# A four-layer selective-scan stack: how the other batch element's steps are dealt out between the scans

## Chip, cores and metric

The kernel runs on one core of a Trainium2 chip. The metric is the device time of one launch in microseconds (us); the time before is the median of three runs. All arithmetic is float32.

## What is computed

Four layers follow each other on x of shape (4, 64, 64, 128): batch, height, width, channels. Layers 0, 1 and 3 are selective-scan blocks, layer 2 is a gated block. Cut to what matters, with L = 4096 positions, DI = 256, N = 16 and four scan directions k (rows, columns, and both backwards):

```
selective-scan block (layers 0, 1, 3)
  xx, z = split(norm(x) @ in_proj)                # 128 -> 256 + 256
  xx    = silu(conv3x3_depthwise(xx) + b)
  for k in 4:  dt, B, C = x_proj[k] @ xs[k];  dt = softplus(dt_w[k] @ dt + b)
               h[t] = exp(dt[t]*A) * h[t-1] + dt[t]*xs[t]*B[t]        # 256 x 16 states
               y[k][t] = sum over n of h[t]*C[t]
  y = sum of y[k], turned back into place, + D * xs
  x = x + (norm(y) * silu(z)) @ out_proj
  x = x + gelu(norm(x) @ fc1 + b) @ fc2 + b       # 128 -> 512 -> 128
gated block (layer 2)
  s = (norm(x) @ w1 + b1) * wdw + bdw;  s = s1 * s2
  s = s * (mean over positions(s) @ wse + bse);   x = x + beta * (s @ w2 + b2)
  c = norm(x) @ wf1 + bf1;                        x = x + gamma * ((c1 * c2) @ wf2 + bf2)
```

## The kernel before, in words

**Turns, chunks, periods.** Elements of the batch go in pairs. While the scans of one element run, everything that is not a scan (norms, projections, convolution, MLP, gated block) is done for the other. There are 12 turns (L709 to L712: element, layer). A turn has 4 directions of 8 chunks of 512 positions, so 32 chunks, and a chunk has 8 periods; the whole is 3072 periods. A period does 4 of the 32 scans of a chunk (16 states for two halves of 128 channels).

**The steady work of a period** is written out by hand in the loop of `scans` (L935 on). In program order: two `da` on ScalarE for the next period (L854, the exponential), two scans on VectorE from `dbp` (L870), the product with C on GpSimd (`hc`, L882) and on every other period a sum of two of them (L884), TensorE's sum over states into `yp` (L895, two or four matmuls, of the period before), TensorE's `dbp` of the next period (L845, four matmuls of 256 columns), two more `da`, then twice a product `dbv` (L984) and a scan on VectorE, a copy `dup` (L862) every other period, and four `diag` on ScalarE (L837) from which a later `dbp` is made. SyncE's queue carries all DMAs; `bb` and `cb`, the rows of B and C, are loaded every other period (L821). PSUM is full: `dbp` has one buffer of two banks, so the next `dbp` can only be written when both its scans are done, and the other element's work has one bank, `gap`.

**Prologue.** The next chunk is prepared by the generator `prologue` (L761 to L814) in ten pieces at fixed half periods (`PIECES`). The piece in the fifth period holds both softplus activations and two table loads on ScalarE.

**The other element's steps.** `between` (L197 on) makes a list of small closures: each issues the instructions of one engine, as a rule. A norm is `mean` (matmul, L226), `centre` (VectorE, L230), `square` (ScalarE, L234), `variance` (matmul, L238), `root` (ScalarE, L241 and L242), `scale` (VectorE, L245), `affine` (ScalarE, L252). The output norm over 256 channels is the same at L338 to L361, `project_z` is L378 to L385, the convolution is nine matmuls for each half (`taps`, L402) with a ScalarE `take` (L413), then `silu` (L421), `gate` on GpSimd (L445), `project` (L450), `add` (L453), the MLP (`up` L477, `take` L480, `gelu` L485, `down` L495, `add` L500), and for the gated layer `product` on GpSimd (L589) and `total` on VectorE (L592). `rest()` puts empty steps (L210) between a producer and its consumer. `later(fn, n)` puts a store n steps further on. In the four turns in which the other element goes through layer 2 (`gated`), three taps make one step:

```python
            stride = 3 if gated else 1
```

**Pacing.** Each period has four places at which `other(number)` issues steps: 0 after the first scan, 1 after the prologue's piece in the middle, 2 after the third scan, 3 at the end. A segment is a list of steps with a first and a last place. Every step counts one, empty ones too, and every place of the segment has the same share:

```python
                gone = at % (8 * per_turn) * 4 + number
                for todo, count, frm, to in segments:
                    while todo and count - len(todo) < count * (gone - frm) / (to - frm):
                        todo.pop(0)()
```

A turn's segment runs from its third period to four places before its 31st chunk (`meanwhile`, L736); so in the last two chunks of a turn nothing of the other element is issued. The first six chunks of the first turn and the last ones of the last turn have a segment for each chunk. What is left at the end is issued after the loop.

Of the kernel before, what the change touches and what calls it, by code (L numbers as in the profile page):

```python
# [58 lines left out]

VSS_AT, VSS_N = _columns(_VSS)  # L60
GATE_AT, GATE_N = _columns(_GATE)


@with_exitstack
def vss_stack_kernel(ctx: ExitStack, tc: tile.TileContext, x: bass.AP, weights, out: bass.AP, n_batch=B, layers=(0, 1, 2, 3)):
# [90 lines left out]
    def combine(i, psums):  # L156

        S = []
        z = SimpleNamespace()

        def load():
            z.in_w = gap1.tile([P, DI], F32, tag="cen", name="in_w")
            nc.sync.dma_start(out=z.in_w, in_=weights[i][0][:, :DI])

        def turn(m):
            z.ps = psums[0].tile([P, CH], F32, tag="gap", name="gap")
            nc.tensor.transpose(z.ps[:, :P], z.in_w[:, m * P : (m + 1) * P], ident)

        def take():
            z.in_t = gap1.tile([P, P], F32, tag="sq", name="in_t")  # L170
            nc.scalar.copy(z.in_t, z.ps[:, :P])

        def taps(m, t, count):
            z.taps = gap1.tile([P, 4, P], F32, tag="t", name="taps")
            for j in range(count):
                nc.scalar.activation(z.taps[:, j], ident, AF.Copy, scale=wt[i]["conv_w"][:, m, t + j : t + j + 1])

        def project(count):
            z.ps = psums[0].tile([P, CH], F32, tag="gap", name="gap")
            for j in range(count):  # L180
                nc.tensor.matmul(z.ps[:, j * P : (j + 1) * P], z.in_t, z.taps[:, j], start=True, stop=True)

        def leave(m, t, count):
            conv = gap1.tile([P, 4 * P], F32, tag="y", name="conv")
            nc.scalar.copy(conv[:, : count * P], z.ps[:, : count * P])
            at = (m * 9 + t) * P
            nc.sync.dma_start(out=conv_d[i][:, at : at + count * P], in_=conv[:, : count * P])

        S.append(load)
        for m in range(2):  # L190
            S.extend((partial(turn, m), take))
            for t in range(0, 9, 4):
                count = min(4, 9 - t)
                S.extend((partial(taps, m, t, count), partial(project, count), partial(leave, m, t, count)))
        return S

    def between(e, frm, to, psums):  # L197
# [9 lines left out]

        def rest(n=pause):

            S.extend([lambda: None] * n)  # L210

        def later(fn, n=3):

# [7 lines left out]

        def norm(src, dst, wgt, bias, eps):

            def mean():
                z.ps = bank()
                nc.tensor.matmul(z.ps, mean128, src(), start=True, stop=True)  # L226

            def centre():
                z.cen = gap1.tile([P, CH], F32, tag="cen", name="cen")
                nc.vector.tensor_sub(z.cen, src(), z.ps)  # L230

            def square():
                z.sq = gap1.tile([P, CH], F32, tag="sq", name="sq")
                nc.scalar.activation(z.sq, z.cen, AF.Square)  # L234

            def variance():
                z.ps = bank()
                nc.tensor.matmul(z.ps, mean128, z.sq, start=True, stop=True)  # L238

            def root():  # L240
                nc.scalar.activation(z.ps, z.ps, AF.Ln, bias=eps)  # L241
                nc.scalar.activation(z.ps, z.ps, AF.Exp, scale=-0.5)  # L242

            def scale():
                nc.vector.tensor_mul(z.cen, z.cen, z.ps)  # L245

            def affine():
                to_sb = dst()
                cen = z.cen
                if len(to_sb.shape) == 3:  # L250
                    cen = cen.rearrange("p (h w) -> p h w", w=W)
                nc.scalar.activation(to_sb, cen, AF.Identity, scale=wgt, bias=bias)  # L252

            S.append(mean)
            rest()
            S.extend((centre, square))
            rest(1)
# [51 lines left out]
        def begin(c):  # L309


            def turn():
# [12 lines left out]
            later(lambda: nc.sync.dma_start(out=lane.res[:, cols(c)], in_=z.res))  # L325

        def output_norm(c):
            if to is None:
                S.append(lambda: fetch(c))
                rest(2)  # L330

            def mean():
# [10 lines left out]
            def square():  # L343
                z.wide = gap1.tile([P, 4, CH], F32, tag="wide", name="wide")
                nc.scalar.activation(z.wide[:, 0:2], z.y, AF.Square)

            def variance():
# [25 lines left out]
            S.append(affine)  # L373

        def project_z():
            def first():
                z.ps = bank()
                nc.tensor.matmul(z.ps, z.in_z[:, :P], z.xn, start=True, stop=True)  # L378

            def second():  # L380
                z.ps = bank()
                nc.tensor.matmul(z.ps, z.in_z[:, P:], z.xn, start=True, stop=True)
# [5 lines left out]

        def convolve(c):

            stride = 3 if gated else 1
            for m in range(2):
                for first in range(0, 9, stride):

                    def taps(m=m, first=first):
                        if m == 0 and first == 0 and (frm is None or gated):
                            z.wide = gap1.tile([P, 4, CH], F32, tag="wide", name="wide")
# [45 lines left out]
        def mixer_out(c):  # L443
            def gate():
                nc.gpsimd.tensor_mul(z.y, z.y, z.wide[:, 0:2])  # L445

            def project():
                z.ps = bank()
                for m in range(2):
# [15 lines left out]
        def mlp(c, store):  # L465
# [4 lines left out]
            norm(lambda: z.res, fresh, v["n2w"], v["n2b"], eps5)  # L470
            for j in range(4):

                def up(j=j):
                    if j == 0:
                        z.wide = gap1.tile([P, 4, CH], F32, tag="wide", name="hid")
# [13 lines left out]
            rest(1 + breath)  # L489
            for j in range(4):  # L490

                def down(j=j):
                    if j == 0:
                        z.ps = bank()
# [48 lines left out]
            later(store, 2)  # L543

        def finish(c):
            def turn():
                z.ps = bank()
                for j in range(4):
# [13 lines left out]
        def gate_sums(c):  # L562
# [6 lines left out]

            norm(lambda: z.res, fresh, g["n1w"], g["n1b"], eps6)  # L570

            def first():
                z.ps = bank()
                nc.tensor.matmul(z.ps, g["w1"][:, :P], z.t, start=True, stop=True)

            def take():
                z.g1 = gap1.tile([P, CH], F32, tag="cen", name="g1")
                nc.scalar.activation(z.g1, z.ps, AF.Identity, scale=g["wdw"][:, 0:1], bias=g["cb"][:, 0:1])

            def second():  # L580
                z.ps = bank()
                nc.tensor.matmul(z.ps, g["w1"][:, P:], z.t, start=True, stop=True)
# [16 lines left out]
        def attention():  # L599
            g = wt[2]  # L600

            def mean():
                z.mean = gap1.tile([P, 1], F32, tag="mean", name="mean")
                nc.vector.tensor_reduce(z.mean, z.sums, AX.X, ALU.add)
                nc.vector.tensor_scalar_mul(z.mean, z.mean, 1.0 / L)

            def se():
                z.ps = bank()
                nc.tensor.matmul(z.ps[:, 0:1], g["wse"], z.mean, start=True, stop=True)
# [10 lines left out]
        def gate_rest(c):  # L620
            g = wt[2]

            def project():
                z.s, z.res = z.next_s, z.next_res
                z.ps = bank()
# [14 lines left out]
            rest(2)  # L640
            norm(lambda: z.res, fresh, g["n2w"], g["n2b"], eps6)

            def first():
                z.ps = bank()
                nc.tensor.matmul(z.ps, g["wf1"][:, :P], z.t, start=True, stop=True)

            def take():
                z.c1 = gap1.tile([P, CH], F32, tag="cen", name="c1")
                nc.scalar.activation(z.c1, z.ps, AF.Identity, bias=g["bf1"][:, 0:1])

            def second():
                z.ps = bank()
                nc.tensor.matmul(z.ps, g["wf1"][:, P:], z.t, start=True, stop=True)

            def both():
                z.c2 = gap1.tile([P, CH], F32, tag="sq", name="c2")
                nc.vector.scalar_tensor_tensor(z.c2, z.ps, g["bf1"][:, 1:2], z.c1, ALU.add, ALU.mult)

            def down():
                z.ps = bank()  # L660
                nc.tensor.matmul(z.ps, g["wf2"], z.c2, start=True, stop=True)
# [94 lines left out]
    def scans(pool, ring, deep, psum):  # L756
# [178 lines left out]
        for at, (s, i) in enumerate(periods):  # L935
            then = periods[at + 1] if at + 1 < len(periods) else None
            if i == 0:
# [2 lines left out]
                    pro, nxt.dt = prologue(nxt), s.dt  # L940
                s.state = pool.tile([P, 2, N], F32, tag="state", name="state") if s.first else before[0].state
                if at % (8 * per_turn) == 0:
                    segments = [(steps, len(steps), frm, to) for steps, frm, to in meanwhile(s.turn)]

            def piece(number):

# [2 lines left out]

            def other(number):  # L950

                gone = at % (8 * per_turn) * 4 + number
                for todo, count, frm, to in segments:
                    while todo and count - len(todo) < count * (gone - frm) / (to - frm):
                        todo.pop(0)()

            da_next = [None, None]
            spreads = (s, i // 2 + 1) if i < 7 else (nxt, 0)
# [46 lines left out]
            da = da_next  # L1005
            before = (s, i)
            if then and then[0].turn != s.turn:
                assert not any(todo for todo, *_ in segments)
# [5 lines left out]
        for todo, *_ in segments:  # L1014
            for step in todo:
                step()

    with (
# [91 lines left out]
```

## Time and profile before

| | us |
|---|---|
| median of three runs (23297.77 to 23323.02) | 23302.88 |
| the profiled execution, its own time | 23325.13 |
| its span, first to last instruction | 23323.4 |
| GpSimd busy | 19260.3 (83%) |
| ScalarE busy | 18075.1 (77%) |
| scans with `dbp` / with `dbv`, mean of one | 1.259 / 1.280 |
| `hc` product on GpSimd, mean of one | 2.361 |
| mean of a period (span without start and end / 3072) | 7.5 |
| mean granted TensorE clock | 0.956 |

The span stretches from the first to the last instruction; the profiled execution's own time is 1.7 us more, and 22 us (0.1%) over the median. A float32 matmul shows as two records. In the views of waits a line says which engine waited with which instruction, what released it, and then the time in total, how often, and the longest.

### The profile page before, as it was taken

To read this page: it belongs to the slowest core of one execution; us is meant where nothing else is said; L and a number is where in the kernel's file an instruction comes from. 1 tells how busy PE (TensorE), PEld (TensorE's weight loads), DVE (VectorE), ACT (ScalarE), POOL (GpSimd) and SP (SyncE) were. 2 spreads that over 40 slices of the span, in tenths; PEclk is the share of its full clock that TensorE was granted. 3 is DMA by queue.
4 is the path that set the end of the run, shared out by engine and by line. 5 is a ranking of instruction groups with operands and counts; after the bars stand their busy time and mean duration, and the time that the engine had idled before them with its cause. 6 is when DMAs were issued, how large, how long until landed. Compare 5 with 4: busy or idle time off the path is not lost. (4 is left out here: it accounts for less than half of the span.)

```text
span 23323.4 us, 216855 instructions
## 1 busy us (share of the span) xinstructions
PE 20052.7 (86%) x58234; PEld 10604.8 (45%) x58234; DVE 20362.5 (87%) x20186; ACT 18075.1 (77%) x38870; POOL 19260.3 (83%) x8862
## 2 busy tenths in 40 slices
PE   7888888888888888888888888888888888888887
PEld 3444444444444444444444444444444444444443
DVE  5999899988887888898899899898988878888996
ACT  5788787777777787787788787787877777877886
POOL 5898888888887787888888788888888878878885
PEclk8999999999999999999999999999999999999998
DMA  4444444444334434434533544444443443344332
GB/s 104 147 142 144 131 130 145 131 131 140 125 125 126 130 126 126 135 130 134 139 133 130 139 138 132 134 144 127 132 141 122 126 128 131 123 128 136 131 132 101
DMA packets 2437558, 3060.09 MB, mean 131 GB/s; under 512 B 1753840, under 2 KB 1790064, under 8 KB 2238192
## 3 DMA queue, kind: packets, MB, share of 16 engines
q1 hardware_dynamic: 2436336, 3046.22, 42.1%
q8 instruction: 472, 7.73, 0.1%
q14 instruction: 750, 6.14, 0.1%
HBM read 2784.41 MB, written 261.49 MB: 131 GB/s over the span
## 5 line engine op out<-in xcount | busy, mean ns | idle before, releaser
L882 POOL TENSOR_TENSOR hc<-h,cb 128x1024 f32<-128x1024 f32 x6144 | 14420.4, 2361 | 3675.8 <-DVE h L870 2362.9
L895 PE MATMUL yp<-hc,ident 128*128 128x512 f32 x18432 | 9087.0, 620 | 641.9 <-POOL hc L884 395.2
L854 ACT ACTIVATE da<-delta,w 128x512 f32<-128x512 f32 x12288 | 8158.8, 713 | 1557.2 <-DVE h L870 1532.3
L845 PE MATMUL dbp<-diag,duT 128*128 128x256 f32 x24576 | 6276.1, 400 | 1832.3 <-DVE h L870 1729.2
L870 DVE TENSOR_TENSOR_SCAN h<-da,state,dbp 128x512 f32<-128x512 f32 x5376 | 6564.8, 1259 | 939.5 <-PE dbp L845 757.6
L870 DVE TENSOR_TENSOR_SCAN h<-da,state,dbv 128x512 f32<-128x512 f32 x5376 | 6879.6, 1280 | 477.6 <-ACT da L854 11.1
L845 PEld LDWEIGHTS dbp<-diag,duT 128*128 128x128 f32 x24576 | 4740.1, 198 | 4329.2 <-issue 2850.9
L895 PEld LDWEIGHTS yp<-hc,ident 128*128 128x128 f32 x18432 | 3491.1, 198 | 4992.6 <-issue 3633.6
L984 DVE TENSOR_TENSOR dbv<-dup,bb 128x512 f32<-128x512 f32 x6144 | 4226.0, 688 | 614.2 <-ACT dup L862 400.7
L837 ACT ACTIVATE diag<-ident,bt 128x128 f32<-128x128 f32 x12288 | 3947.5, 401 | 0.2
L884 POOL TENSOR_TENSOR hc<-hc 128x1024 f32<-128x1024 f32 x1536 | 3622.5, 2358 | 120.4
L862 ACT COPY dup<-du 128x512 f32<-128x512 f32 x1920 | 1125.3, 586 | 1267.6 <-DVE dbv L984 1231.8
L402 PE MATMUL gap<-halo,cw 128*128 128x512 f32 x3456 | 1658.6, 605 | 15.6 <-ACT wide L413 6.2
L870 DVE TENSOR_TENSOR_SCAN h<-da,dbp 128x512 f32<-128x512 f32 x768 | 892.5, 1200 | 130.8 <-PE dbp L845 104.1
L870 DVE TENSOR_TENSOR_SCAN h<-da,dbv 128x512 f32<-128x512 f32 x768 | 937.3, 1220 | 79.3 <-ACT da L854 14.1
L805 POOL TENSOR_TENSOR du<-delta,xs 128x512 f32<-128x512 f32 x768 | 978.3, 1274 | 33.7 <-ACT delta L793 33.7
L788 PE MATMUL ps_dt<-xd,dt_w 8*128 8x512 f32 x1536 | 887.2, 658 | 124.9 <-ACT delta L791 73.6
L402 PEld LDWEIGHTS gap<-halo,cw 128*128 128x128 f32 x3456 | 642.1, 192 | 743.8 <-issue 700.7
L878 ACT COPY state<-h 128x2 f32<-128x2 f32 x5376 | 960.9, 179 | 0.0
L413 ACT ACTIVATE wide<-gap,w 128x512 f32<-128x512 f32 x192 | 132.1, 688 | 824.2 <-PE gap L402 824.1
L813 ACT COPY duT<-ps_duT 128x512 f32<-128x512 f32 x768 | 440.0, 573 | 181.3 <-PE ps_duT L811 180.5
L791 ACT ACTIVATE delta<-ps_dt,w 128x512 f32<-128x512 f32 x768 | 524.6, 683 | 37.2 <-PE ps_dt L788 32.6
(121 smaller groups left out, 11443.0 us busy)
## 6 DMA issues: line engine op xcount, KB each, us to landing
cb<-xd_d SPq DMA_DIRECT2D x1536, 1024.0 KB
bb<-xd_d SPq DMA_DIRECT2D x1536, 512.0 KB
xs<-x_row_d SPq DMA_DIRECT2D x192, 512.0 KB
xs<-x_col_d SPq DMA_DIRECT2D x192, 512.0 KB
x_col_d<-down SPq DMA_DIRECT2D x192, 256.0 KB
x_row_d<-wide SPq DMA_DIRECT2D x96, 512.0 KB
y_d<-y_sb SPq DMA_DIRECT2D x96, 512.0 KB
y<-y_d SPq DMA_DIRECT2D x96, 512.0 KB
```

Of the source, the lines that this page charges most:

```text
L402: nc.tensor.matmul(z.ps, z.cw[:, m, t, :], z.halo[c][:, dy : dy + RPC, dx : dx + W], start=(t == 0), stop=(t == 8),)
L805: nc.gpsimd.tensor_mul(s.du[:, m], s.delta[:, m], s.xs[:, m])
L837: nc.scalar.activation(s.diag[q][:, t, :, j], ident, AF.Copy, scale=s.bt[:, t, CQ * q + j : CQ * q + j + 1])
L845: nc.tensor.matmul(s.db[:, t * P : (t + 1) * P, :], s.duT[:, t, m, :], s.diag[q][:, t], start=True, stop=True)
L854: nc.scalar.activation(da[:, j], s.delta[:, m], AF.Exp, scale=s.v["a"][:, s.k, m, n : n + 1])
L862: nc.scalar.copy(s.dup, s.du[:, m])
L870: nc.vector.tensor_tensor_scan(s.h[i, side][:, j, s.step], da[:, j, s.step], db[:, s.step], init, ALU.mult, ALU.add)
L878: nc.scalar.copy(s.state[:, m, n : n + 2].unsqueeze(2), s.h[i, side][:, :, s.end : s.end + 1])
L882: nc.gpsimd.tensor_mul(hc, s.h[i, side], s.cb[i // 2][:, 2 * side : 2 * side + 2, :])
L884: nc.gpsimd.tensor_add(hc, hc, s.hc[i, 0])
L895: nc.tensor.matmul(getattr(s, f"yp{m}"), ident, s.hc[i, side][:, j], start=opens and j == 0, stop=i == end and side == 1 and j == 1,)
L984: nc.vector.tensor_mul(db, s.dup, s.bb[i // 2][:, j])
```

## The change

1. A decorator `tensor(n)` marks a step with its number of 512-column matmuls: 1 for `mean`, `variance`, `first`, `second`, `up`, `down` and single taps; 2 for the output norm's `mean` and `variance` and for `project`; 0.6 for four transposes, 0.3 for smaller ones, 0.1 for `se`.
2. A step costs that many; an empty step costs 0.1, any other step 0.25. A segment advances by cost and no longer by number of steps.
3. The places of a chunk no longer have equal shares: the eight periods have the shares of `ROOM`, each spread evenly over its four places.
4. Taps are single steps in all turns (`stride = 1`).
5. At one place a segment issues either steps with matmuls or steps without; when the kind changes it stops until the next place, unless the segment's end has been reached. Empty steps have no kind.

The lists of steps and their order within a segment stay as they were, but for the split taps. The instructions on every engine are the same ones in another order between the scans.

```diff
+ROOM = (0.8, 1.9, 1.0, 0.9, 0.2, 0.4, 0.9, 1.2)
+
+def tensor(matmuls):
+    def mark(fn):
+        fn.matmuls = matmuls
+        return fn
+    return mark
+
+def cost(step):
+    return getattr(step, "matmuls", 0) or (0.1 if step is empty else 0.25)
+
+def when(place):
+    chunk, place = divmod(place, 4 * len(ROOM))
+    i, number = divmod(place, 4)
+    return chunk + (sum(ROOM[:i]) + ROOM[i] * number / 4) / sum(ROOM)
...
-            S.extend([lambda: None] * n)
+            S.extend([empty] * n)
...
+            @tensor(1)
             def mean():
...
-            stride = 3 if gated else 1
+            stride = 1
             for m in range(2):
                 for first in range(0, 9, stride):
+                    @tensor(stride)
                     def taps(m=m, first=first):
...
-                    segments = [(steps, len(steps), frm, to) for steps, frm, to in meanwhile(s.turn)]
+                    segments = [
+                        SimpleNamespace(todo=steps, done=0.0, total=sum(map(cost, steps)), frm=when(frm), to=when(to))
+                        for steps, frm, to in meanwhile(s.turn)
+                    ]
...
-                gone = at % (8 * per_turn) * 4 + number
-                for todo, count, frm, to in segments:
-                    while todo and count - len(todo) < count * (gone - frm) / (to - frm):
-                        todo.pop(0)()
+                gone = when(at % (8 * per_turn) * 4 + number)
+                for g in segments:
+                    last = None
+                    while g.todo and g.done < g.total * (gone - g.frm) / (g.to - g.frm):
+                        step = g.todo[0]
+                        kind = None if step is empty else hasattr(step, "matmuls")
+                        if None not in (kind, last) and kind != last and gone < g.to:
+                            break
+                        last = last if kind is None else kind
+                        g.done += cost(g.todo.pop(0))
+                        step()
```

More of the change, by code (lines that the diff above doesn't have):

```diff
@@ L61, with empty @@
 GATE_AT, GATE_N = _columns(_GATE)
+ROOM = (0.8, 1.9, 1.0, 0.9, 0.2, 0.4, 0.9, 1.2)
[6 more added lines that the diff above has]
+    return getattr(step, "matmuls", 0) or (0.1 if step is empty else 0.25)
+def empty():
+    pass
+def when(place):
+    chunk, place = divmod(place, 4 * len(ROOM))
+    i, number = divmod(place, 4)
+    return chunk + (sum(ROOM[:i]) + ROOM[i] * number / 4) / sum(ROOM)
 @with_exitstack
@@ L190, in combine @@
         for m in range(2):
-            S.extend((partial(turn, m), take))
+            S.extend((tensor(0.3)(partial(turn, m)), take))
             for t in range(0, 9, 4):
                 count = min(4, 9 - t)
-                S.extend((partial(taps, m, t, count), partial(project, count), partial(leave, m, t, count)))
+                S.extend((partial(taps, m, t, count), tensor(0.3 * count)(partial(project, count)), partial(leave, m, t, count)))
         return S
@@ L234, in square @@
                 nc.scalar.activation(z.sq, z.cen, AF.Square)
+            @tensor(1)
             def variance():
@@ L309, in begin @@
         def begin(c):
+            @tensor(0.6)
             def turn():
@@ L330, in output_norm @@
                 rest(2)
+            @tensor(2)
             def mean():
@@ L345, in square @@
                 nc.scalar.activation(z.wide[:, 0:2], z.y, AF.Square)
+            @tensor(2)
             def variance():
@@ L375, in project_z @@
         def project_z():
+            @tensor(1)
             def first():
@@ L378, in first @@
                 nc.tensor.matmul(z.ps, z.in_z[:, :P], z.xn, start=True, stop=True)
+            @tensor(1)
             def second():
@@ L445, in gate @@
                 nc.gpsimd.tensor_mul(z.y, z.y, z.wide[:, 0:2])
+            @tensor(2)
             def project():
@@ L471, in mlp @@
             for j in range(4):
+                @tensor(1)
                 def up(j=j):
@@ L490, in mlp @@
             for j in range(4):
+                @tensor(1)
                 def down(j=j):
@@ L545, in finish @@
         def finish(c):
+            @tensor(0.6)
             def turn():
@@ L570, in gate_sums @@
             norm(lambda: z.res, fresh, g["n1w"], g["n1b"], eps6)
+            @tensor(1)
             def first():
@@ L578, in take @@
                 nc.scalar.activation(z.g1, z.ps, AF.Identity, scale=g["wdw"][:, 0:1], bias=g["cb"][:, 0:1])
+            @tensor(1)
             def second():
@@ L605, in mean @@
                 nc.vector.tensor_scalar_mul(z.mean, z.mean, 1.0 / L)
+            @tensor(0.1)
             def se():
@@ L621, in gate_rest @@
             g = wt[2]
+            @tensor(1)
             def project():
@@ L641, in gate_rest @@
             norm(lambda: z.res, fresh, g["n2w"], g["n2b"], eps6)
+            @tensor(1)
             def first():
@@ L649, in take @@
                 nc.scalar.activation(z.c1, z.ps, AF.Identity, bias=g["bf1"][:, 0:1])
+            @tensor(1)
             def second():
@@ L657, in both @@
                 nc.vector.scalar_tensor_tensor(z.c2, z.ps, g["bf1"][:, 1:2], z.c1, ALU.add, ALU.mult)
+            @tensor(1)
             def down():
@@ L1007, in scans @@
             if then and then[0].turn != s.turn:
-                assert not any(todo for todo, *_ in segments)
+                assert not any(g.todo for g in segments)
         save(*before, 1)
@@ L1013, in scans @@
             leave(*full.pop(0))
-        for todo, *_ in segments:
-            for step in todo:
+        for g in segments:
+            for step in g.todo:
                 step()
```

## The prediction

> **What bounds the kernel now.** I read the busy rows first, then the windows of single chunks, then the waits of ScalarE and VectorE, then one stretch of the timeline.
>
> ```profile
> PE 20052.7 (86%) x58234; PEld 10604.8 (45%) x58234; DVE 20362.5 (87%) x20186; ACT 18075.1 (77%) x38870; POOL 19260.3 (83%) x8862
> ```
>
> Four engines lie between 77% and 87%, so no single one is the bound and what matters is how long they wait for each other. The windows are a chunk without the other element's work (the last of a turn), one with norm and MLP only, and one of a gated turn with convolution; the second set is TensorE's work into `gap` alone.
>
> ```profile
> core 0: us, PE busy (x) PEld busy (x) DVE busy (x) ACT busy (x) POOL busy (x), PEclk, DMA share, GB/s
> 9718.90:9771.30 52.40, 43.95 (x132) 23.68 (x132) 50.72 (x51) 39.20 (x81) 49.11 (x24) 0.97 0.43 144
> 2171.50:2226.90 55.40, 46.83 (x143) 24.20 (x141) 53.72 (x54) 48.15 (x105) 48.53 (x28) 1.00 0.38 131
> 9049.90:9126.30 76.40, 67.69 (x178) 34.39 (x178) 52.98 (x53) 50.12 (x108) 49.55 (x23) 0.90 0.42 98
> ...
> core 0: us, PE busy (x), PEclk, DMA share, GB/s
> 9718.90:9771.30 52.40, 0.00 (x0) 0.97 0.43 144
> 2171.50:2226.90 55.40, 5.80 (x12) 1.00 0.38 131
> 9049.90:9126.30 76.40, 23.78 (x46) 0.90 0.42 98
> ```
>
> The quiet chunk is VectorE's (50.7 of 52.4 us, 6.55 us a period). The convolution's chunk takes 24 us more with VectorE no busier: that is TensorE. Over all 3072 periods the excess above quiet ones is about 2740 us, of which 760 are VectorE's own extra instructions; some 2000 us are waiting.
>
> ```profile
> ACT wide L413 <- PE gap L402: 824.1, 180, 10.7
> ACT gap L241 <- PE gap L238: 297.7, 137, 5.3
> ...
> DVE h L870 <- PE dbp L845: 861.7, 417, 10.8
> DVE dbv L984 <- ACT dup L862: 400.7, 205, 5.5
> DVE cen L245 <- ACT gap L242: 262.2, 140, 10.7
> ```
>
> and how they hang together, inside that chunk:
>
> ```profile
> 9069.09 5.32 PE L402 MATMUL gap<-halo,cw 128*128 128x512 f32 x12
> ...
> 9074.25 1.89 PE L845 MATMUL dbp<-diag,duT 128*128 128x256 f32 x8
> ...
> 9074.44 0.69 ACT L413 ACTIVATE wide<-gap,w 128x512 f32<-128x512 f32 x1 [6.81 <-PE gap L402]
> ...
> 9076.27 2.45 DVE L870 TENSOR_TENSOR_SCAN h<-da,state,dbp 128x512 f32<-128x512 f32 x2 [6.29 <-PE dbp L845]
> ```
>
> Twelve records, six taps, stand ahead of `dbp` on TensorE; ScalarE's `take` waits 6.8 us for the last of them with all that ScalarE has to do behind it, and VectorE waits 6.3 us for `dbp`.
>
> **What the change takes away.** No instruction is added or removed; I counted each place's steps from the order of both programs. A tap is two records of 0.43 us (12 in 5.15 us when they follow closely), so a triple step is 2.6 us and a single one 0.86. Before, a convolution ran one step a place, four taps a period, up to twelve in gated turns. After, at most 1.05 taps a place in the second period of a chunk and about two a period on average. Periods with more than 3.5 matmuls of the other element fall from 239 to 80; the fullest chunk from 33 to 21. The pile-ups are priced from two sides.
>
> Lower end: TensorE's steady work of a period is 3.4 to 6.1 us (records of 0.43 and 0.214 us). Adding the other element's, the sum over periods of what exceeds 7 us falls from 857 to 532: 325 us.
>
> Upper end: the rows of ScalarE. `take` stood one place after the last tap 141 times and waited 4.7 us, two places after it 36 times and waited 1.2. After, it stands one place behind 52 times and two or more 136 times, with no row of taps before the last: 0.4 us each, about 80 in place of 824. `root` waits 403 us for its variance now (297.7 and 105.1 for the wide norm); at one place of distance 1.1, at two 0.3. After, the distance is two or more 123 times of 250 and 89 times of 95: about 165, so 240 less. A least-squares fit of the excess of 375 chunks on these waits gives 0.67 us of time for each us that ScalarE waits for TensorE, 0.62 for each that VectorE waits on the other element's steps, 0.15 for TensorE's. 0.67 x (744 + 240) = 660 us.
>
> I take **500**: between both, since the fit counts some pile-ups twice.
>
> **What it costs.** Empty steps shrink from one place to 0.1, so producers and consumers move together.
> - `root` to `scale` (ScalarE to VectorE): in the same place 134 + 29 times of 345 (8 before), one place apart 106 + 58. Where ScalarE stands when VectorE reaches a place follows from `da`, state copies and `diag`: +0.65, -0.54, +0.15, +0.58 us for places 0 to 3 (medians). With `root` at 0.656 + 0.582 us VectorE waits 0.8 to 2.0 us, with ScalarE's late cases **2.0** on average. The rows: 1.4 at one place, and 4.9 and 3.1 at none (four cases each, mostly in the crowded last turn). Ends 0.8 and 4.9; I take 2.0 as it follows from the durations. 163 x 2.0 + 164 x 0.7 = 441, against 342 now (262.2 and 79.8): +99.
> - `mean` to `centre` (TensorE to VectorE): one place in 97 cases, where two was the least and three to five the rule. A mean at place 1 comes after `dbp` on TensorE, 2.9 us behind the second scan, and VectorE is at place 2 after 2.0: 0.8 us each, ends 0 and 2.4 (the wide norm's row at two places). +85, and +35 for the wide norm.
> - `product` to `total` (GpSimd to VectorE): same place 20 times of 32, one place 8; two places waited 2.45 us each. GpSimd has an `hc` of 2.36 us ahead: 5.5 us. +72. Other adds: +30.
>
> VectorE: 321 x 0.62 = **199**.
> - `gate` to `project`: one place 76 times of 95. TensorE waited 0.9 us at two places; a place is 1.9 us: +200 us on TensorE, behind which stand `yp` or `dbp`. x 0.15 = 30.
> - `centre` and `square` in one place, 190 times: ScalarE waits 0.8 to 1.1 for VectorE, +80 x 0.67 = 54, and behind it wait the next `da`.
> - SyncE: `x_row` is stored one or two places after `silu` (four before), `store` 0 or 1 after its copy (two before). The queue then stands before the loads of `bb` and `cb`, whose landings cost 112.8 us on VectorE and 395.9 on GpSimd now. Ends 0 and 200 (half as much again on GpSimd, all of it passed on); 50, as most loads have a period of lead. The fetch after `project` moves from one place behind it to three or more, which can only help.
> - Nine more steps are left for the end: under 5 us.
>
> Sum 333. Net 500 - 333 = 167 us less.
>
> **The clock, where a rule speaks against the change.** The trace has 2070 us at half clock (0.956 on average), mostly windows of 3.4 us, in the first, second, fourth and sixth period of a chunk above all. The shares 0.2 and 0.4 take matmuls out of the fifth and sixth period: 0.55 in place of 1.34 and 1.22. The Trainium skill, "TensorE: Matmul & The Clock Gate", section "Why this matters for your kernels", says that gaps in TensorE's work of over about 3 us bring it back to half clock, so these holes should cost. By the rule, one more cold window of 3.4 us in each of 384 chunks makes TensorE 384 x 1.7 = 650 us slower in its own time, x 0.15 = 100 us here. By the trace, half-clock time in the fifth period is 0.49, 0.74, 0.37, 0.69 us with 0, 1, 2, 3 or more matmuls of the other element, in the sixth 0.75, 1.00, 1.09, 0.53: it does not follow them, since `yp` and `dbp` go on in each. Carried over to the changed loads it gives 1896 us for 1960 within the periods. I take zero; 100 goes into the range.
>
> **Rivals.**
> 1. *Pile-ups go, hand-offs cost as priced* (0.46): 23303 - 167 = 23136, about **23140**, within 22960 and 23255.
> 2. *Hand-offs are hidden* (0.14): ScalarE is less late everywhere once convolutions don't hold it, so the places without distance cost little; 500 to 660 less 100: 22,740 to 22,900. For it: 0.67 is the largest factor of the fit. Against it: `root` to `scale` at one place already waits.
> 3. *They cancel* (0.13): pile-ups at the lower end, 325 - 333: 23310.
> 4. *Slower, VectorE waits on `root` in the same place* (0.27). With the price of the four rows, 4.9 us, VectorE's additional wait is 163 x 4.9 - 5 = 794 us, x 0.62 = 492; with the other 134 that is 626 against 500: +126, 23,430; with the pile-ups at 325, 23,600. It decides from 3.65 us per hand-off (0.62 x (163 x 3.65 - 5) = 366 = 500 - 134). For it: ScalarE is over 4 us late in a tenth of the places. Against it: that lateness comes from the convolutions' `take` and the fifth period, which the change relieves.
>
> That the change does not do what it says I leave out: in the order of the changed program the taps do stand singly and paced, and only ten places (the end of four early and six late segments) release five or nine steps at once.
>
> **How the numbers follow.** The range goes from 22,770 (gain at its upper end, hand-offs at 134) to 23,480 (rival 4 and half of its lower gain). What a measurement of this kernel can tell from no change is about 0.2%, 47 us: 23,256 to 23,349. Faster is the first two cases but for 0.01 at the edge, 0.59; same 0.14; slower 0.27.
>
> **What would show it.** Right: `wide` waiting for `gap` (824) under 200 us, scans waiting for `dbp` under 600, chunk windows with convolution under 65 us; `cen` waiting for `root` at 350 to 500; `sums` over 130. Wrong: `cen` waiting over 800, or `dup` and `da` waits of VectorE growing (ScalarE as the late one), or the wait for `dbp` unchanged, which would mean that `dbp` is late because of `yp` and not of taps; and half-clock time above 2700 us would mean that the rule of the clock holds here.

## Result and profile after

The changed kernel takes **23554.24 us** (median of four runs, 23543.04 to 23573.13), against 23305.42 for the kernel before on the same chip: a ratio of 1.0107, 95% interval 1.0089 to 1.0124. That is about 250 us slower, where 167 us faster was forecast, and above the range's upper end of 23,480. The profiled execution took 23543.04 us, its span is 23541.3.

The busy row of the changed kernel's page:

```profile
PE 20110.0 (85%) x58234; PEld 10601.3 (45%) x58234; DVE 20360.2 (86%) x20186; ACT 18131.1 (77%) x38870; POOL 19261.7 (82%) x8862
```

Counts are the same and busy times within 60 us of before: all of the difference is waiting. The windows of three chunks of the changed kernel (quiet, norm and MLP, and the convolution's chunk at the place shown for before):

```profile
core 0: us, PE busy (x) PEld busy (x) DVE busy (x) ACT busy (x) POOL busy (x), PEclk, DMA share, GB/s
9820.60:9873.30 52.70, 44.36 (x133) 23.50 (x134) 50.66 (x51) 39.20 (x80) 49.40 (x23) 0.97 0.41 143
2208.60:2269.90 61.30, 51.02 (x151) 26.87 (x150) 54.42 (x55) 50.30 (x109) 50.83 (x24) 0.97 0.36 127
9191.20:9263.20 72.00, 56.66 (x156) 29.37 (x156) 54.20 (x56) 52.80 (x112) 52.64 (x27) 0.91 0.51 122
```

The convolution's chunk fell from 76.4 to 72.0 us; the chunk with norm and MLP took 61.3 us where before's took 55.4 (with 18 records into `gap`, where that had 12). What moved is in the waits. ScalarE's rows for the last tap and for the variance, then VectorE's list, after the change:

```profile
ACT wide L451 <- PE gap L440: 203.5, 95, 9.6
...
ACT gap L273 <- PE gap L270: 138.5, 67, 9.5
```
```profile
DVE h L919 <- PE dbp L894: 679.7, 331, 7.9
DVE cen L277 <- ACT gap L274: 399.5, 176, 13.0
DVE cen L261 <- PE gap L257: 323.9, 93, 31.4
DVE res L541 <- PE gap L536: 171.5, 26, 22.2
DVE dbv L1044 <- ACT dup L911: 165.0, 119, 4.5
DVE res L492 <- PE gap L489: 132.7, 33, 13.4
DVE sums L636 <- POOL g L633: 130.0, 32, 6.4
```

The pile-ups shrank: `take` waits 203.5 us for the taps (824.1 before), the scans 679.7 for `dbp` (861.7), `dbv` 165.0 for `dup` (400.7). In their place VectorE waits for the other element's own chain: `centre` for `mean` (L261) 323.9 us where it was 64.3, the two adds (L541, L492) 304.2 where they were 78.2. These rows before:

```profile
DVE sums L592 <- POOL g L589: 78.6, 28, 4.6
DVE y L341 <- PE gap L338: 66.6, 17, 8.1
...
DVE cen L230 <- PE gap L226: 64.3, 17, 31.8
DVE res L500 <- PE gap L495: 50.4, 12, 21.4
...
DVE res L453 <- PE gap L450: 27.8, 7, 13.5
```

Summed over the waits of more than 0.15 us (VectorE's from the first scan on; the last row is the first experiment below):

| us | scans wait | VectorE waits on the other element's steps | ScalarE waits for TensorE |
|---|---|---|---|
| before | 1627 | 564 | 2161 |
| after | 1150 | 1271 | 1308 |
| difference | -477 | +707 | -853 |
| after, with equal shares | 1178 | 990 | 1251 |

VectorE is busy as long as before, so its two columns must add up to about the difference of the spans: +230 us and 218. One place shows how the waits come about, inside a gated turn of the changed kernel (start, duration, engine, line; the idle time before it in brackets):

```profile
8227.91 1.26 DVE L919 TENSOR_TENSOR_SCAN h<-da,state,dbp 128x512 f32<-128x512 f32 x1
8228.10 1.28 ACT L459 ACT_TABLE_LOAD   x1
...
8229.39 1.06 ACT L459 ACTIVATE wide<-wide 128x1024 f32<-128x1024 f32 x1
...
8230.53 2.35 POOL L483 TENSOR_TENSOR y<-y,wide 128x1024 f32<-128x1024 f32 x1 [3.51 <-ACT wide L459]
...
8232.93 3.66 PE L489 MATMUL gap<-y,pw 128*128 128x512 f32 x4 [2.04 <-POOL y L483]
...
8236.63 0.69 DVE L492 TENSOR_TENSOR res<-res,gap 128x512 f32<-128x512 f32 x1 [7.46 <-PE gap L489]
8237.23 1.27 DVE L919 TENSOR_TENSOR_SCAN h<-da,state,dbp 128x512 f32<-128x512 f32 x1
```

`silu`, `gate`, `project` and `add` stand in neighbouring places of the same program order, one on each of four engines. Each engine reaches its step and finds the one before it unfinished. The add stands ahead of the next scan in VectorE's order, so the scans stand still for 7.5 us, and this period lasts 17.5 us where the mean is 7.5. Each gated turn has one such wait of this add, of 7.0 to 7.5 us.

Part of it is TensorE's clock. TensorE had been idle for 2.04 us, and the four records of `project` took 3.66 us at half clock, where four records of `yp` take 1.88. The first view has the granted clock of this stretch as PEclk, 0.53; the second has the rows of `project` before and after (busy us, mean ns of a record, idle time before):

```profile
core 0: us, PE busy (x) PEld busy (x) DVE busy (x) ACT busy (x) POOL busy (x), PEclk, DMA share, GB/s
8232.93:8236.59 3.66, 3.66 (x5) 1.67 (x6) 0.00 (x0) 1.90 (x5) 2.25 (x1) 0.53 0.00 0
```
```profile
L450 PE MATMUL gap<-y,pw 128*128 128x512 f32 x384 | 217.8, 696 | 51.2 <-POOL y L445 51.0
...
L489 PE MATMUL gap<-y,pw 128*128 128x512 f32 x384 | 285.7, 886 | 236.7 <-POOL y L483 236.7
```

By period of the chunk (a period counted from its first scan, summed over the run) the difference is +13, +79, +546, +16, -4, -315, -214, +84 us: the third period pays more than the sixth and seventh give back. By turn it is +35 in the first, +135 in the four gated turns, +27 in the last, and within 6 us each way in the other plain turns. The gated turns gain in their convolution part and lose in the rest: before, 154 periods up to the first tap had a mean of 7.75 us and 102 from it on 8.23; after, 130 have 8.35 and 126 have 7.78.

### The profile page after: what moved, and what is told of

Read it like the earlier page. It is cut to its first block, busy times and chain, and to the rows that moved or that the text cites. A ratio compares the mean times of both kernels' runs of the same rounds, so it can differ in the third digit from the quotient of the medians.

```text
span 23541.3 us, 216613 instructions
## 1 busy us (share of the span) xinstructions
PE 20110.0 (85%) x58234; PEld 10601.3 (45%) x58234; DVE 20360.2 (86%) x20186; ACT 18131.1 (77%) x38870; POOL 19261.7 (82%) x8862
## 5 line engine op out<-in xcount | busy, mean ns | idle before, releaser
L1044 DVE TENSOR_TENSOR dbv<-dup,bb 128x512 f32<-128x512 f32 x6144 | 4224.9, 688 | 379.3 <-ACT dup L911 165.0
L440 PE MATMUL gap<-halo,cw 128*128 128x512 f32 x3456 | 1749.8, 606 | 8.5 <-DVE cen L277 3.7
L536 PE MATMUL gap<-hid,pw 128*128 128x512 f32 x768 | 425.2, 658 | 158.6 <-ACT hid L525 158.6
L277 DVE TENSOR_TENSOR cen<-cen,gap 128x512 f32<-128x512 f32 x256 | 174.5, 682 | 399.8 <-ACT gap L274 399.5
```

Source lines behind the costliest of these rows:

```text
L440: nc.tensor.matmul(z.ps, z.cw[:, m, t, :], z.halo[c][:, dy : dy + RPC, dx : dx + W], start=(t == 0), stop=(t == 8),)
L1044: nc.vector.tensor_mul(db, s.dup, s.bb[i // 2][:, j])
```

## Experiments

Two theories stood at first. The first says that distance is the cause: empty steps that cost 0.1 bring producer and consumer together. The second says that the shares of `ROOM` are: the rest of the steps is squeezed into too few periods. Edits are against the changed kernel unless said otherwise, and where a cut shows only a + line, it replaces the line that the change has there. Each ratio is to the kernel before, timed beside it on the same chip; its medians lay between 23299.93 and 23313.53, so that differences between experiments are good to some 15 us.

**Equal shares.**
```diff
-ROOM = (0.8, 1.9, 1.0, 0.9, 0.2, 0.4, 0.9, 1.2)
+ROOM = (0.9125,) * 8
```


> The changed kernel with equal shares for the eight periods of a chunk (0.9125 each), all else as changed. Theory H (hand-offs too close: VectorE waits 700 us more on the other element's steps): mean to centre moves from one place apart in 97 cases to 31, project and down to add move away too, root to scale stays (130 in one place for 163), so about 23,300 (-250 against the changed kernel). Theory R (the shares and the rule of one kind crowd 2.0 matmuls into the third period, which has 6.0 us of TensorE's steady work; the third period is 546 us longer in sum): third period back from 8.63 to about 7.3 us, but fifth and sixth lose their relief of 530 in part, 23,050 to 23,250.

23297.76, ratio 0.9997 (0.9989 to 1.0006): 256 us less than the change. With equal shares the rest of the change does nothing measurable to the time. The scans wait as under the change; it is VectorE's waits on the other element's steps that fall, by 281 us, but not back to where they were before:

```profile
DVE h L919 <- PE dbp L894: 526.8, 275, 16.7
DVE cen L277 <- ACT gap L274: 317.6, 171, 10.6
...
DVE cen L261 <- PE gap L257: 253.8, 93, 32.0
...
DVE res L492 <- PE gap L489: 111.3, 28, 13.4
...
DVE res L541 <- PE gap L536: 84.7, 27, 21.8
```

**No rule of kinds.**
```diff
-                        if None not in (kind, last) and kind != last and gone < g.to:
+                        if False:
```


> The changed kernel without the rule of one kind of step in a place. Then ScalarE's, VectorE's or GpSimd's step may stand in the same place as the matmul before it, but steps are not put off into the third period (1.78 matmuls there for 2.00, 2.30 in the second for 1.97) and mean to centre is one place apart 46 times for 97. Theory H: gate to project falls into one place 30 times, mean to centre improves: within 100 of the changed kernel, 23,450 to 23,550. Theory R: third period 0.5 us shorter, 23,350.

23488.74, 1.0080 (1.0065 to 1.0095): the rule costs about 65 us.

**Longer rests.**
```diff
-    return getattr(step, "matmuls", 0) or (0.1 if step is empty else 0.25)
+    return getattr(step, "matmuls", 0) or (0.5 if step is empty else 0.25)
```


> The changed kernel with an empty step at a cost of 0.5 for 0.1, so that a rest of three is again about three places. Shares as changed, third period still 2.1 matmuls. Theory H: mean to centre one place apart 41 for 97, adds further away; root to scale is not helped (174 in one place): VectorE's waits on the other element's steps fall by 250, 23,300. Theory R: no gain, 23,550 or more, as periods with more than 3.5 matmuls rise from 80 to 148.

23539.75, 1.0102 (1.0087 to 1.0117): no change in time. VectorE's waits in this run:

```profile
DVE h L919 <- PE dbp L894: 818.8, 377, 10.1
DVE cen L277 <- ACT gap L274: 347.5, 159, 11.5
DVE dbv L1044 <- ACT dup L911: 273.5, 132, 5.6
DVE cen L261 <- PE gap L257: 216.2, 68, 31.3
```

The two `cen` rows fall by 160 us, and the rows of `dbp` and `dup` rise by 248. Over all rows, waits on the other element's steps fall by 265 and those of the scans rise by 255. Rests that take up share leave less of it for the other steps, which crowd more (argued). Longer distances alone don't bring the time back.

**Single taps alone**, in the kernel before:
```diff
-            stride = 3 if gated else 1
+            stride = 1
```


> The kernel before with single taps in gated turns, nothing else. Pile-ups of six taps ahead of dbp go in four turns, but a step still counts one and 384 steps more quicken the pace of all others there. Both theories: 23,150 to 23,250 (-50 to -150 against before); if single taps were a part of the loss, over 23,350.

23265.83, 0.9983 (0.9977 to 0.9990): a gain of 40 us.

**Shares after TensorE's free time.** TensorE's mean busy time in the eight periods of quiet chunks (the last two of a turn) is 6.26 4.27 6.85 5.54 6.46 4.08 5.91 3.63 us; the shares follow its complement.
```diff
+ROOM = (0.5, 1.5, 0.4, 1.3, 0.3, 1.2, 0.5, 1.6)
```


> The changed kernel with shares that follow TensorE's steady work: ROOM (0.5, 1.5, 0.4, 1.3, 0.3, 1.2, 0.5, 1.6), much in the second, fourth, sixth and eighth period, where two sums fewer into yp stand; third period 1.29 matmuls for 2.00. The hand-offs stay as close as in the changed kernel (mean to centre one place apart 80 times for 97, root to scale in one place 182 for 163, and far closer than with equal shares: 31 and 130). Theory R (crowding): no slower than equal shares, 23,100 to 23,300. Theory H (hand-offs): as slow as the changed kernel, 23,450 to 23,550.

23323.96, 1.0009 (1.0002 to 1.0016): shares as unequal as the change's cost 26 us more than equal ones, where the change's cost 256. Being unequal is not enough.

**Third share cut**, then **second share cut**:
```diff
+ROOM = (0.8, 1.9, 0.1, 0.9, 0.2, 0.4, 0.9, 1.2)
```


> The changed kernel with one number changed: the third period's share is 0.1 for 1.0, which brings its matmuls from 2.00 to 1.35 and the second's from 1.97 to 2.20. Hand-offs are closer still (mean to centre one place apart 119 times). Theory R: the third period's sum loses most of its 546 us, about 200 of it net, 23,300 to 23,400. Theory H: slower than the changed kernel, 23,600.

23499.52, 1.0081 (1.0066 to 1.0097). The third period has nearly no share, but still gets 1.35 of the other element's matmuls (2.00 under the change), and it is still 460 us longer in sum than before. That it pays for what was issued in the second is likely, but not shown.

```diff
+ROOM = (0.8, 0.9, 1.0, 0.9, 0.2, 0.4, 0.9, 1.2)
```


> The changed kernel with only the second period's share changed, 0.9 for 1.9; the second and third period then get 1.46 and 1.68 matmuls for 1.97 and 2.00, the fifth and sixth keep their small shares (0.66 and 0.60). Cutting the third's share alone had left the third period 460 us longer in sum, so theory R now says that the engines come out of the crowded second period behind and the third can't catch up: third period under 7.6 us, 23,300 to 23,380. If the small shares of the fifth and sixth are what costs (the work has to go somewhere), 23,450 or more.

23511.29, 1.0089 (1.0072 to 1.0106). The third period is still 253 us longer, and the first and last now pay more. So the large second share isn't the cause by itself either.

**The shares alone**: all of the change but the shares is taken back, which makes it the kernel before with the shares of `ROOM`:
```diff
-    return getattr(step, "matmuls", 0) or (0.1 if step is empty else 0.25)
+    return 1.0
...
-            stride = 1
+            stride = 3 if gated else 1
...
-                        if None not in (kind, last) and kind != last and gone < g.to:
+                        if False:
```


> The kernel before in all but the shares: every step counts one, triple taps in gated turns, no rule of kinds, but the eight periods have the shares of ROOM. Second and third period get 2.42 and 1.86 matmuls, periods with more than 3.5 rise to 246, at most 15. Theory R: the shares alone make it slower by as much as the whole change or more, 23,550 to 23,800, the third period longer by 400 and more in sum. If the loss came from counting by matmuls or from the rule of kinds, about 23,300.

23646.65, 1.0145 (1.0130 to 1.0160): +344 us. The shares do it without the costs and without short rests. Here both sums rise over those of before: scans 1627 to 1716, other steps 564 to 803.

**Equal shares with longer rests** (the first and the third edit together):
```diff
+ROOM = (0.9125,) * 8
+    return getattr(step, "matmuls", 0) or (0.5 if step is empty else 0.25)
```


> Equal shares and empty steps at 0.5: mean to centre one place apart 11 times for 31, two places 12 for 104, gate to project one place 39 for 89, root to scale in one place 106 for 130. Theory H: VectorE's waits on the other element's steps (about 1000 us with equal shares) fall by 250 and the time with them, 23,050 to 23,150. Theory R: those waits fall, but scans wait more in their place, as in the kernel with long rests and the shares as changed; 23,250 to 23,300.

23379.23, 1.0033 (1.0020 to 1.0045), 81 slower than equal shares with short rests: waits on the other element's steps 990 to 776, those of the scans 1178 to 1456. Longer distances alone don't gain here either.

**Fifth and sixth raised:**
```diff
+ROOM = (0.8, 1.9, 1.0, 0.9, 0.9, 0.9, 0.9, 1.2)
```


> The changed kernel with the shares of the fifth and sixth period raised to 0.9; the second keeps 1.9 and gets 1.75 matmuls, the third 1.66. Theory R (the second period's crowd): part of the loss stays, 23,400 to 23,480. If the emptied fifth and sixth are the cause: 23,300.

23314.21, 1.0006 (0.9997 to 1.0014): the loss is gone, with the second share still at 1.9. In the change the harm hangs on the small shares of the fifth and sixth.

**Equal shares, no rule of kinds:**
```diff
+ROOM = (0.9125,) * 8
+                        if False:
```


> Equal shares and no rule of one kind: counting by matmuls alone. Mean to centre is two or more places apart always (one place 31 times with the rule), periods with more than 3.5 matmuls 4 for 14. With the shares as changed, dropping the rule gave 65 us. Theory R: the rule matters little when nothing is crowded, 23,250 to 23,300; if the rule itself puts steps off into bad places, 23,150 to 23,230.

23251.84, 0.9976 (0.9968 to 0.9984): 46 us less than with the rule, which agrees with the 65 above.

**Every step counts, taps double**, with equal shares and no rule of kinds (the second + line is shortened to what it returns):
```diff
+ROOM = (0.9125,) * 8
-    return getattr(step, "matmuls", 0) or (0.1 if step is empty else 0.25)
+    return 2.0 if getattr(step, "tap", False) else 1.0
...
+                    taps.tap = True
+                        if False:
```


> Equal shares, no rule of kinds, single taps that count two, every other step, the empty ones too, one. The convolution runs at two taps a period as in the change (periods with more than 3.5 matmuls 46 for 239) and the rests stay about as long as before (mean to centre never under two places, root to scale in one place 44 for 163). If pile-ups of taps cost what their waits showed before, and close hand-offs cost what theirs show now, both gains add: 22,950 to 23,150. If waits at either place only show lateness that comes back elsewhere, 23,230 to 23,300.

23143.70, 0.9932 (0.9917 to 0.9947): **faster than both kernels**, by 161 us than before. It differs from single taps alone (23265.83) only in that a tap counts two, so 122 of the 161 us come from that weight. Its waits on VectorE:

```profile
DVE h L920 <- PE dbp L895: 574.0, 317, 11.6
DVE dbv L1045 <- ACT dup L912: 328.3, 191, 5.1
DVE cen L277 <- ACT gap L274: 286.3, 133, 10.7
```

The `dbp` row is below the changed kernel's and the `cen` row is near before's (262.2): over all rows scans 1262, other steps 743. Against before it gains 22 to 36 us in each plain turn but the first (16 more) and the last (9 less).

**Two neighbours emptied**, the other six equal:
```diff
+ROOM = (1.117, 1.117, 1.117, 1.117, 0.2, 0.4, 1.117, 1.117)
```


> Equal shares of 1.117, but 0.2 and 0.4 for the fifth and sixth period as in the change (0.66 and 0.54 matmuls there, 1.4 to 1.7 elsewhere). Theory U (taking work out of the fifth gives nothing back, the others pay): 23,450 to 23,550, the fifth period as long as before. If it is the second period's 1.9 after all: 23,300.

23541.41, 1.0098 (1.0083 to 1.0113), +244 to equal shares.

```diff
+ROOM = (1.117, 1.117, 0.2, 0.4, 1.117, 1.117, 1.117, 1.117)
```


> The control: equal shares of 1.117, but 0.2 and 0.4 for the third and fourth period (0.79 and 0.55 matmuls). If any two emptied periods cost alike, as no period falls under the scans' own 6.4 us: 23,450 to 23,550. If the fifth and sixth are special: 23,250 to 23,350, since work taken from in front of the prologue's piece leaves ScalarE on time for it.

23510.58, 1.0084 (1.0069 to 1.0099), +213. Both pairs that were tried cost nearly the same.

**One of them raised** in the changed kernel:
```diff
+ROOM = (0.8, 1.9, 1.0, 0.9, 0.9, 0.4, 0.9, 1.2)
```


> The changed kernel with the fifth period's share at 0.9 for 0.2 and the sixth's left at 0.4: 1.20 matmuls in the fifth for 0.55. Theory U with the fifth as the period that gives nothing back: most of the loss goes, 23,350 to 23,400. If the sixth is as important: half, 23,430.

23473.54, 1.0067 (1.0051 to 1.0084), -81.

```diff
+ROOM = (0.8, 1.9, 1.0, 0.9, 0.2, 0.9, 0.9, 1.2)
```


> The changed kernel with the sixth period's share at 0.9 for 0.4 and the fifth's left at 0.2: 0.92 matmuls in the sixth for 0.54. The sixth did become shorter by being emptied (7.57 to 6.75 us), so theory U expects little from giving it work again: 23,480 to 23,530; if both are alike, 23,430.

23330.82, 1.0006 (0.9998 to 1.0015), -223: nearly the whole loss. This suggested that the sixth, in which TensorE has little steady work, is the period one must not empty. The next two test that.

**One period emptied**, seven equal:
```diff
+ROOM = (1.014, 1.014, 1.014, 1.014, 1.014, 0.2, 1.014, 1.014)
```


> Equal shares of 1.014, the sixth period alone at 0.2 (0.64 matmuls for 1.25). Theory T: 23,400 to 23,480, nearly all in the four gated turns. If a single emptied period of any kind is harmless: 23,300.

23317.62, 1.0008 (1.0000 to 1.0017), +20 to equal shares.

```diff
+ROOM = (1.014, 1.014, 0.2, 1.014, 1.014, 1.014, 1.014, 1.014)
```


> Equal shares of 1.014, the third period alone at 0.2 (0.69 matmuls for 1.32), the one in which TensorE has the most steady work. Theory T: 23,250 to 23,320, as with equal shares. If emptying any period costs alike: the same as with the sixth emptied.

23323.71, 1.0008 (0.9999 to 1.0017), +26. Emptying one period costs little, the sixth (4.08 us of TensorE's steady work) no less than the third (6.85). The idea that TensorE's room decides falls.

## Why the prediction was wrong

**What held.** *What bounds*: no engine's work changed, and VectorE's waits account for the time. *The pile-ups' waits*: ScalarE's two rows that were priced, `take` and `root`, wait 851 us less (984 were named), and the scans wait 477 less. That 500 us of time went with them is not shown: no run gained as much, the best one 161. Three signs named for "right" were missed, though not by far: the taps' row is 203.5 (under 200 was asked), the row of `dbp` 679.7 (under 600), the convolution's chunk 72.0 us (under 65). None of the signs named for "wrong" came.

**The step that failed is the cost in VectorE's waits**, the 321 in "321 x 0.62 = 199": VectorE waited 707 us more for the other element's steps. Term by term, from the rows of both kernels:

- `root` to `scale`: +99 forecast; 399.5 + 46.0 against 262.2 + 79.8 is +103.5. In the same place the wait was 2.4 us (2.0 taken), 134 times. Right. This was also the place of rival 4, whose sign was right and whose mechanism wasn't: its 4.9 us per hand-off did not occur.
- `mean` to `centre`: +120 forecast; 323.9 and 109.6 (the wide norm) against 64.3 and 66.6 is **+303**. At one place it was 2.16 us each (97 cases) where 0.8 was taken, and at two places 0.85 (85 cases), where before had 0.07. 2.4 had been named as the upper end and set aside. Of the 323.9 us, 249 stand in the four gated turns.
- adds: "+30" in a clause; 304.2 against 78.2 is **+226**. No working stood behind the 30. `gate` to `project` was followed to TensorE, whose wait came as forecast (+186 for +200), and weighted by 0.15; but the `add` behind `project` stands ahead of a scan. Over one to three places' distance it waited 7.4 to 2.8 us in 25 cases. Of all adds, 109 us stand in the last turn.
- `product` to `total`: +72 forecast, +51. SyncE's queue: 50 us of time taken; VectorE's wait for `bb` went from 112.8 to 114.8, GpSimd's for `cb` from 395.9 to 489.2.
- The factor 0.62 can't be judged. VectorE's waits together must give the difference of the times, but a single group of rows need not: longer rests took 265 us out of this group, and the time stayed. With 707 in place of 321 and all else as forecast, the net is 500 - 438 - 134, which is 72 us slower. The other 177 us of the measured 249 have no term of their own.

The upper end of the range doesn't follow from its working either: rival 4's 23,430 and half of its lower gain of 175 is 23,517 and not 23,480. The result lies above both.

**Two errors, not one.** Between the forecast and the result lie 416 us, and equal shares split them. From before to equal shares, the scans wait 449 us less and VectorE waits 426 more on the other element's steps: the time stays, where 167 less was forecast. So the hand-offs cost more than priced even without unequal shares (46 us of this time are the rule of kinds). From equal shares to the change, the scans wait 28 us less and the other waits grow by 281: the time grows by 256. The prediction saw in the shares only fewer full periods (239 to 80), a count of matmuls, and priced each place by its mean lateness in the kernel before.

**What the cause is, as far as shown.** Shown: the change is slower than before because of its shares, not because of single taps (-40 alone) and only by 46 to 65 us because of the rule of kinds. The way is also shown: twelve kernels differ in `ROOM` alone, and in all of them the scans wait 1104 to 1192 us. VectorE's waits on the other element's steps are 990 to 1076 us in the six that lie within 33 us of equal shares, and 1166 to 1284 in the six that are 176 to 256 us slower. Two neighbouring periods emptied cost 213 to 244, a single one 20 to 26; whether two that aren't neighbours would cost as much was not tried.

*The clock, put at zero.* Half-clock time rose from 2070 to about 2270 us, under the 2700 named, and with equal shares it is 2412 at the time of before, so its sum doesn't order the times. Where it falls is another matter. Of VectorE's waits for TensorE, 139 us lay in half-clock windows before, 393 with equal shares, 485 after and 164 with the shares alone. A record of `project` takes 0.59 us at full clock and 1.22 at half, so about half of these waits at most is the clock's. By that estimate, from their own length alone, it makes up to 127 us of the first error, but only 46 of the 256 us that the shares cost, and 13 of the 344 with the shares alone. So the clock is hardly what makes the shares slow; its part in the first error stays open, and zero was not shown.

Only argued: that levelling TensorE's work unlevels the rest. Under the change TensorE's work of the other element is more even between periods (its standard deviation falls from 1.34 to 0.91 us), while the sum over TensorE, ScalarE and VectorE is less even (1.86 to 1.96), because steps without matmuls cost nearly nothing and come in bursts. Over all 20 kernels this sum's spread goes with the time (correlation 0.82; TensorE's own 0.31), but it was worked out afterwards, and it has exceptions: before has 1.86 at 23305 us, the fifth raised 1.78 at 23474, the sixth raised 1.84 at 23331.

**Open**: why raising the sixth alone undoes nearly all and the fifth alone a third. The difference of the two lies in the four gated turns, which are 118 us longer than before with the fifth raised and 37 us shorter with the sixth raised. Nor are neighbours the whole story: with the fifth raised only the sixth has a small share (0.4), as in the kernel with the sixth alone emptied (0.2), and still it takes 156 us more than that one.

## What to carry to other kernels

When work is dealt out between the steps of a tight loop on several in-order engines, weigh the heavy steps, but let the light ones and the rests keep their count: with taps at double weight and every other step at one, the gain was 0.7%; counting by matmuls, with equal shares and no rule of kinds, it was 0.2%. Unequal shares that left two neighbouring stretches nearly empty lost about 1% here. Price a hand-off at the row of its own distance, and follow it to the engine on which the main chain waits. Don't add up the rows of an engine's waits as if they were separate gains: what leaves one row can come back in another.

## What the hardware showed beyond that

Less granted clock didn't mean a longer time: with equal shares the mean clock was 0.948 at 23298 us, with the change 0.952 at 23554, with the sixth raised 0.956 at 23331.

The clock is granted in windows of 3.41 us. After the first 200 us, every window that follows one in which TensorE's records (whose ends the profile models) leave 2.1 us or more idle is at half clock (343 of 343 before, 374 of 374 after). Of some 6190 windows at full clock in each profile, none follows one with over 2.02 us idle. So the rule that the prediction cites from the Trainium skill, "TensorE: Matmul & The Clock Gate", section "Why this matters for your kernels", with its gaps of over about 3 us, holds in this case from about 2 us on; the 2.04 us in front of `project` were enough.
